# A relational graph layer: the first block keeps its edges, types come by marks, and the bias lies in PSUM

## The chip, the cores and the metric

The kernel runs on one core of one Trainium2 chip, in one launch. The metric is the device time of that launch in microseconds (us), a median of several runs; lower is better. TensorE (PE) multiplies matrices, VectorE (DVE) works elementwise, ScalarE (ACT) applies functions, GpSimd (POOL) here issues the gathers, and SyncE (SP) issues the other transfers.

## The reference

There are N = 12,500 nodes with 256 features each, E = 212,500 edges sorted by their target, and R = 8 relation types. Each node has one edge to itself, and it is the last of the node's edges in the sorted order.

```python
h   = relu(layernorm(x))                      # [12500, 256]
hx  = einsum('ni,rio->rno', h, weight)        # a 256x256 weight for each type
msg = hx[edge_type, src]
agg = segment_sum(msg, dst, num_segments=12500)
out = x + agg * sqrt(0.5) + h_bias + (h @ loop_weight) * sqrt(0.5)
```

## The kernel before

**Order of the sums.** The kernel sums first and multiplies later: for each type r and node d it adds the rows h[src] of the edges of that type, and then multiplies the eight sums of a node by the eight weights. The sums lie transposed in SBUF in `acc`, [128 features, 2 halves, 8 types, a ring of 768 nodes]. A *group* is 128 nodes; the ring has six slots (`SLOTS`), and 98 groups pass through it. Four groups make a quad (`XG = 4`), in which rows are loaded and stored.

**Tiles and units.** Edges are cut, in their order, into 796 units of 267 (`EDGES`). A unit takes two tiles (`PAIR`) of 128 message slots, 256 in all. It holds 267 edges because last edges that are self edges need no slot: they are taken out of the list (*compaction*), as their message is the node's own row. 128 units form a block (*b*, 7 of them), whose indices are prepared together, one unit per partition. `prepare(b)` lists the steps: `load_indices` (three transfers on SP: `nat_s`, `nat_d`, `nat_t`), `sources` (compaction in five rounds of two DVE operations, L331 and L332, then the transposed gather indices `gidx`), `last_edges` (the types of the last edges, compacted to the front in nine rounds: `loops`), `columns` (the column that each edge adds into) and `places`. These steps are put in a list called `background`, and some of them are taken from it at each tile.

**The main loop over 1592 tiles.** The order of the work on each engine is written out by hand. At tile t the loop issues `gather(t + 58)` on POOL (L607: 128 rows by index from HBM into `msg`, a buffer of 31 pairs of tiles), makes one-hot matrices for later tiles on DVE (L620: `oh` compares `cols` with a row of numbers), multiplies message by one-hot on PE (`edge_sums`, L647, two products of 32-bit floats, each of two instructions), and adds a unit's result into `acc` on DVE (`add_sums`, L659, at an offset held in a register).

**Rows.** Before it can gather from h, the kernel normalizes all rows (`norm_rows`, pieces of four times 128 rows: moments on DVE at L555 and L557, scaling on ACT at L567, then a store to h). Four pieces go ahead of the loop, the others in its first 28 tiles, three in four tiles. The first 96 tiles gather from x, and their messages are normalized as they come (`moments` with "e_").

**Groups.** When a group's last unit is in, `group_work(g)` puts 18 products (a self product and eight types, two halves each: L758, 36 instructions) and ahead of them a bias product (L752: a row of ones times `bias_in`) into a queue that is spread over the coming tiles. `finish()` then adds x (L767), stores a quad's output, and calls `begin(g + 6)`: two transposes of the new group's rows on PE (L671), a copy on ACT (`self_t`, L674), and eight DVE operations (L679) that set each type's columns of the slot to the row where the node's last edge has that type, and to zero elsewhere. `begin` thus both clears the slot and adds the last edges.

**Types.** `find_types(q)` gets, for a quad, the type of each node's last edge onto all 128 partitions. For each block that can touch the quad it makes one matrix of places on DVE (L698), and multiplies it by 22 columns of `loops`, each shifted by one (L701: 22 products of 128x512 elements for each block, 44 where two blocks touch the quad). ACT copies the result to `types` (L706). The transposes, the products for types and the turned indices share one PSUM bank, `ptt`, `pst` and `ptr` by name. Ahead of the loop the kernel runs block 0's preparation, `find_types` for the first two quads, and six `begin`s.

Of the kernel before, what the change touches and what calls it, by code (L numbers as in the profile page):

```python
# [28 lines left out]
EDGES = 267  # L29

# [6 lines left out]
SLOTS = 6  # L37
RING = GROUP * SLOTS

# [21 lines left out]
PREP = 300  # L61
STEP = 3
# [5 lines left out]
class Plan:  # L68
# [5 lines left out]

    def __init__(self, N, E):
        U = EDGES
        self.NU = NU = -(-E // U)
        self.NT = NU * PAIR - (1 if E - (NU - 1) * U <= P else 0)
        slack = 6.5 * (E / 4) ** 0.5 / U + 1.0
        self.rate = rate = E / (N * U)  # L80

        self.low = [(1 / rate, -slack / rate), (1.1 / rate, -(1.5 + 0.1 * E / U) / rate)]
        self.high = [(1 / rate, slack / rate)]
        self.starts = list(range(0, N, GROUP))
        self.ends = self.starts[1:] + [N]
        self.NG = len(self.starts)
        self.last = [
            min([NU - 1, *(int((e + 2 - b) / a) + 1 for a, b in self.low)]) for e in self.ends]
        self.last[-1] = NU - 1

        self.begin = lambda u: max(0.0, *(a * u + b for a, b in self.low))
        self.blocks = [
            [b for b in range(-(-NU // P))
             if self.begin(b * P) <= e + 2
             and self.high[0][0] * min(NU - 1, b * P + P - 1) + self.high[0][1] + 2 * WIN + 2 >= s]
            for s, e in zip(self.starts[::XG], self.starts[XG::XG] + [N])]
        a, b = self.high[0]
        self.first = [max(0, int((s - WIN - 2 - b) / a) - 1) if s else 0 for s in self.starts]
# [102 lines left out]
def kernel(  # L201
# [23 lines left out]
    EU = E - (NU - 1) * EDGES  # L225
    NB = -(-NU // P)

    TB, SB = (R - 1).bit_length(), (WIN - 1).bit_length()
# [12 lines left out]
    bias_in = const.tile([1, D], F32, name="bias_in")  # L241
    one = const.tile([1, P], F32, name="one")
# [5 lines left out]
    line = const.tile([P, XG * GROUP + WIN - 1], F32, name="line")  # L248
# [9 lines left out]
    with ExitStack() as main:  # L258
# [11 lines left out]

        selves = main.enter_context(tc.tile_pool(name="selves", bufs=SLOTS + 1))
# [9 lines left out]
        ps_o = main.enter_context(tc.tile_pool(name="ps_o", bufs=2, space=PSUM))  # L281
        msg, oh, offsets, kind = {}, {}, {}, {}
        firsts, loops, typed, gidx, col = {}, {}, {}, {}, {}
        added, begun = {}, set()
# [3 lines left out]
        def load_indices(b):  # L288
            rows_ = min(P, NU - b * P)
            last = b == NB - 1  # L290
            full = rows_ - last
            e0 = b * P * EDGES
            nat = {}
            for name, a, more in (("s", src, 0), ("d", dst, 1), ("t", etype, 0)):
                n = ep.tile([P, EDGES + more], I32, name=f"nat_{name}")
                if last:
# [4 lines left out]
                    else:  # L301
                        nc.vector.memset(n, 0)
                if full:
                    nc.sync.dma_start(n[:full, :], bass.AP(
                        tensor=a.tensor, offset=a.offset + e0, ap=[[EDGES, full], [1, EDGES + more]]))
# [21 lines left out]
        def compacted(got, bit, bits):  # L327

            def step(k):
                m = work_tile(got, "moves", 6, I32)  # L330
# [6 lines left out]
        def sources(b, got):  # L337


# [15 lines left out]
            def codes():  # L355
                nc.vector.scalar_tensor_tensor(
                    got["code"], got["code"], float(R), got["t"], op0=ALU.mult, op1=ALU.add)

            def packs():
                nc.vector.scalar_tensor_tensor(  # L360
                    packed, got["s"], float(1 << (TB + SB)), got["code"],
                    op0=ALU.mult, op1=ALU.add)

            def unpacks():
                nc.vector.tensor_single_scalar(
                    work_tile(got, "from", 6, I32)[:, :U], packed[:, :U], TB + SB,
# [11 lines left out]
        def last_edges(b, got):  # L378

            def selves_():  # L380
                nc.vector.tensor_tensor(
                    work_tile(got, "same", 4), got["s"], got["d"][:, :EDGES], op=ALU.is_equal)

            def ends():
                nc.vector.scalar_tensor_tensor(
                    work_tile(got, "end", 5), got["rise"], 1.0, got["same"],
# [7 lines left out]
            def codes():  # L394
                nc.vector.scalar_tensor_tensor(
                    got["rise"], got["rise"], -2.0 * R, got["t"], op0=ALU.mult, op1=ALU.add)
# [6 lines left out]
            def number():  # L403
                got["ends"] = small.tile([P, 1], F32, name="ends")
                nc.vector.tensor_reduce(got["ends"], got["end"], AX.X, ALU.add)

            def kept():
                nc.vector.tensor_single_scalar(
                    work_tile(got, "kinds", 6, I32)[:, :WIN], packed[:, :WIN], 2 * R - 1,
                    op=ALU.bitwise_and)  # L410
                loops[b] = small.tile([P, WIN], BF16, name="loops")
                nc.vector.scalar_tensor_tensor(
                    loops[b], line[:, :WIN], got["ends"], got["kinds"][:, :WIN],
                    op0=ALU.is_lt, op1=ALU.mult)

            return [selves_, ends, moves, codes, packs, number,
                    *compacted(got, TB + 1, (EDGES - 1).bit_length()), kept]

        def columns(b, got):
# [4 lines left out]
            def bases():  # L424
                got["base"] = small.tile([P, 1], F32, name="base")
                nc.vector.tensor_scalar(
                    got["base"], firsts[b], low[:, b : b + 1], high[:, b : b + 1],
                    op0=ALU.max, op1=ALU.min)

# [48 lines left out]
            def all_():  # L478
                nc.vector.scalar_tensor_tensor(
                    got["valid"], got["ends"], float(WIN), got["valid"], op0=ALU.min, op1=ALU.add)  # L480
                nc.vector.tensor_tensor(
                    counts[:, b : b + 1], got["valid"], got["fit"], op=ALU.mult)

            return [bases, offs, fits, number, there, moved, to, final, valid, sum_, all_,
# [95 lines left out]
        def norm_rows(i):  # L580
# [4 lines left out]
            def rest():  # L585
                after()
                nc.sync.dma_start(rows_of(h32, i), xt[:n, :k, :])
                for g in range(d // P, min(d // P + k, SLOTS, plan.NG)):
                    begin(g, xt[:, g - d // P, :])
# [65 lines left out]
        def add_sums(u, ps):  # L655
# [5 lines left out]

            assert all(g in begun for g in range(plan.NG) if plan.first[g] <= u)


        def begin(g, rows_):

            n = plan.ends[g] - plan.starts[g]
# [322 lines left out]
```

## Time and profile before

| | |
|---|---|
| Median of 3 runs | 2237.54 us (2236.86 to 2239.26) |
| Profiled execution | 2238.67 us |
| Its span on the core | 2236.7 us |
| Mean granted TensorE clock | 0.94 |
| Instructions | 30,467 |
| Bytes moved | 279.14 MB, of which 208.77 MB by the gathers' queue |
| First gather starts | 13.15 us |
| First edge product starts | 83.83 us |
| Bias load issued (all rows normalized) | 187.20 us |
| Last gather starts | 2151.26 us |

The page of a profile has the busy time of each engine, the chain of work that ended last followed back from the end, and the costliest groups of instructions by line: their busy time, the mean ns of one, and, behind the bar, the idle time of the engine just before them with what ended it. Lines of the timeline give a start, a duration, the engine, the line, output and inputs, and in brackets the idle time ahead with its releaser. Lines of the windows view give a stretch of time, its length, the busy time of PE, PE's weight loads, DVE, ACT and POOL, then the granted TensorE clock, the mean share of the transfer queues and GB/s. Idle time marked "issue" is time in which the engine waited for nothing that the profile shows.

### The profile page before, as it was taken

How to read it: one execution, taken by the hardware profiler on the slowest of the kernel's cores; microseconds unless marked ns; L12 is line 12 of the kernel's file. 1: busy time of each engine (PE TensorE's matmuls, PEld its weight loads, DVE VectorE, ACT ScalarE, POOL GpSimd, SP SyncE). 2: the span in 40 equal slices, each digit the busy share in tenths (PEclk: the TensorE clock that was granted, in tenths of full speed). 3: DMA queues.
4: the chain of work that ended last, by engine and by line, in shares of the span. 5: the costliest groups of instructions: out<-in, count | busy, mean ns of one | idle time of the engine just before them, and what ended most of it. 6: DMA issues, size and time to landing. Idle time of an engine off the chain costs nothing.

```text
span 2236.7 us, 30467 instructions
## 1 busy us (share of the span) xinstructions
PE 1984.4 (89%) x11073; PEld 1699.8 (76%) x11073; DVE 1290.3 (58%) x3124; ACT 170.4 (8%) x373; POOL 1512.0 (68%) x1618
## 2 busy tenths in 40 slices
PE   2236899999999999999999999999999799999999
PEld 1235788787787787797787797787797687897897
DVE  6787754485464485454584454684455475564552
ACT  1465300000000000000000000000000000000000
POOL 6624677676777677776777776777777576777730
PEclk9556999999999999999999999999999899999999
DMA  4785344343344344344343443444344343443420
GB/s 133 227 277 183 90 132 135 96 133 117 110 133 132 99 134 121 113 133 118 114 134 108 125 134 103 135 133 119 115 135 120 94 130 96 134 133 101 129 68 14
DMA packets 145685, 279.14 MB, mean 125 GB/s; under 512 B 27909, under 2 KB 94590, under 8 KB 145534
## 3 DMA queue, kind: packets, MB, share of 16 engines
q0 software_dynamic: 76416, 208.77, 32.3%
q1 hardware_dynamic: 69118, 68.40, 9.6%
q8 instruction: 90, 1.47, 0.3%
q14 instruction: 61, 0.50, 0.1%
HBM read 251.46 MB, written 25.60 MB: 124 GB/s over the span
## 4 chain that ended last, share of the span: by engine, by line
PE 78%; DVE 13%; issue 3%; ACT 2%; POOL 1%; DMA 1%; DVEq 0%; SPq 0%; ACTq 0%; POOLq 0%
PE ps L647 34%; PE po L758 31%; PE ptt L701 9%; DVE acc L679 4%; PE po L752 2%; DVE oh L620 1%; POOL msg L607 1%; DVE acc L659 1%; DVE moves L331 1%; PE pst L671 1%; DVE fixed L332 1%; DVE e_stats L555 1%; DVE n_stats L555 1%; ACT xt L567 1%; ACT self_t L674 0%
## 5 line engine op out<-in xcount | busy, mean ns | idle before, releaser
L607 POOL DMA_INDIRECT msg<-h,gidx x1496 | 1417.4, 947 | 544.8 <-issue 405.9
L647 PE MATMUL ps<-oh,msg 128*128 128x176 f32 (+1 forms) x6368 | 1103.7, 305 | 79.9 <-ACT msg L567 51.7
L647 PEld LDWEIGHTS ps<-oh,msg 128*128 128x128 f32 x6368 | 1028.6, 194 | 154.3 <-ACT msg L567 54.8
L758 PE MATMUL po<-w,acc 128*128 128x256 f32 x3136 | 870.2, 380 | 0.8 <-DVE flag L521 0.8
L620 DVE TENSOR_TENSOR oh<-fixed,cols 128x704 f32<-128x704 f32 x398 | 353.3, 888 | 445.4 <-PE ps L647 439.9
L659 DVE TENSOR_TENSOR acc<-acc,ps 128x352 f32 x796 | 409.3, 514 | 285.4 <-PE ps L647 278.9
L758 PEld LDWEIGHTS po<-w,acc 128*128 128x128 f32 x3136 | 531.8, 190 | 22.8 <-issue 1.0
L679 DVE SCALAR_TENSOR_TENSOR acc<-types,pst 128x256 f32<-128x256 bf16 (+1 forms) x784 | 267.5, 413 | 113.7 <-ACT self_t L674 113.7
L701 PE MATMUL ptt<-places,loops 128*128 128x512 bf16 (+1 forms) x748 | 210.7, 452 | 95.6 <-DVE places L698 94.9
L701 PEld LDWEIGHTS <-loops 128*128 128x128 bf16 x748 | 83.3, 114 | 217.2 <-DVE places L698 99.1
L674 ACT ACTIVATE self_t<-pst 128x256 f32<-128x256 f32 x98 | 37.4, 382 | 1578.5 <-PE pst L671 1578.5
L607 POOL DMA_INDIRECT msg<-in_x_dram,gidx x96 | 92.3, 962 | 94.7 <-issue 60.7
L758 PE MATMUL po<-wl,self_t 128*128 128x256 f32 x392 | 111.7, 408 | 0.0
L758 PEld LDWEIGHTS po<-wl,self_t 128*128 128x128 f32 x392 | 66.7, 190 | 38.2 <-issue 32.9
L752 PE MATMUL po<-bias_in,one 1*128 1x256 f32 x196 | 68.6, 429 | 0.9 <-DVE xr L767 0.9
L567 ACT ACTIVATE xt<-xt,n_shift,n_rstd 128x256 f32<-128x256 f32 x98 | 51.0, 589 | 29.8 <-DVE n_shift L564 29.8
L567 ACT ACTIVATE msg<-msg,e_shift,e_rstd 128x256 f32<-128x256 f32 x96 | 49.8, 589 | 13.4 <-DVE e_shift L564 13.4
L752 PEld LDWEIGHTS po<-bias_in,one 1*128 1x128 f32 x196 | 28.9, 184 | 23.3 <-issue 21.4
L767 DVE TENSOR_TENSOR xr<-xr,po 128x256 f32<-128x256 f32 x98 | 40.3, 412 | 9.1 <-PE po L758 8.7
L331 DVE TENSOR_SCALAR moves<-fixed 128x267 int32<-128x267 int32 x98 | 42.3, 431 | 2.1
L332 DVE COPY_PREDICATED fixed<-moves,fixed 128x266 int32<-128x266 int32 (+6 forms) x98 | 39.3, 401 | 3.4
L706 ACT ACTIVATE types<-ptt 128x512 bf16<-128x512 f32 (+1 forms) x25 | 14.7, 587 | 322.7 <-PE ptt L701 322.7
(92 smaller groups left out, 327.5 us busy)
## 6 DMA issues: line engine op xcount, KB each, us to landing
msg<-h,gidx POOLq DMA_INDIRECT x1496, 2.8
xt<-in_x_dram SPq DMA_DIRECT2D x24, 512.0 KB, 6.2
h<-xt SPq DMA_DIRECT2D x24, 512.0 KB, 3.8
xr<-in_x_dram SPq DMA_DIRECT2D x24, 512.0 KB, 7.7
out_dram<-xr SPq DMA_DIRECT2D x24, 512.0 KB, 3.6
hr<-h SPq DMA_DIRECT2D x23, 512.0 KB, 5.2
w<-in_L_gnn_weight_dram SPq DMA_DIRECT2D x2, 1024.0 KB, 5.9
msg<-in_x_dram,gidx POOLq DMA_INDIRECT x96, 2.9
```

Source lines behind the costliest of these rows:

```text
L331: nc.vector.tensor_single_scalar(m, packed, 1 << (bit + k), op=ALU.bitwise_and)
L332: nc.vector.copy_predicated(packed[:, : EDGES - (1 << k)], m[:, 1 << k :], packed[:, 1 << k :])
L555: nc.vector.bn_stats(stats[:n, j, :], rows_[j])
L567: nc.scalar.activation(rows_[j], rows_[j], AF.Relu, bias=shift[:n, j : j + 1], scale=rstd[:n, j : j + 1])
L607: nc.gpsimd.indirect_dma_start(out=msg[t], out_offset=None, in_=table[:, :], in_offset=bass.IndirectOffsetOnAxis(ap=gidx[b][:, at : at + 1 ...
L620: nc.vector.tensor_tensor(o[:, k : k + v, :i, :], iota_f.unsqueeze(1).unsqueeze(1).to_broadcast([P, v, i, C]), of.unsqueeze(3).to_broadcas ...
L647: nc.tensor.matmul(ps[:, c, from_ : from_ + width], m[:, c * P : (c + 1) * P], o[:, :width], start=(i == 0 and c == 0), stop=(end and c == ...
L659: i = nc.vector.tensor_tensor(a, a, ps, op=ALU.add)
L679: i = nc.vector.scalar_tensor_tensor(acc[:, :, r, s0 : s0 + n], of, float(r + 1), pst[:, :, :n], op0=ALU.is_equal, op1=ALU.mult)
L701: nc.tensor.matmul(pt[:, :n], loops[b][:, k : k + 1].to_broadcast([P, P]), o[:, WIN - 1 - k : WIN - 1 - k + n], start=(b == bs[0] and k == ...
L752: nc.tensor.matmul(got["out", g][:n], one[:, :n], bias_in, start=True, stop=False)
L758: i = nc.tensor.matmul(got["out", g][:n], lhs, rhs, start=False, stop=(r == R - 1 and c == KC - 1))
```

## The change

It has five parts.

1. Block 0 keeps all its edges: its units hold 256 edges, and self edges are gathered as all others are. No compaction, no last edges and no types are needed for it. There are then 802 units and 1603 tiles.
2. Quads that only block 0 can touch (the first three, `plan.typed = 3`) get no `begin`. Their slots of `acc` are cleared on ACT (`clear`; three ahead of the loop, three in its first tiles, six later), and their rows are loaded from h and transposed for the self product shortly before it (`turn_nodes`).
3. For the later quads, `mark` makes for each block two step functions over the quad's 512 nodes (from the first node of a unit, from the node behind its last). `find_types` multiplies them, as weights, by 24 columns (22 types and the unit's first node in two parts), 8 products for a block; six small DVE operations pick each node's type out of the result, and ACT scales the identity by it. Three tiles later `spread_types` multiplies a matrix of ones by this diagonal: one product of 128x512.
4. The bias is loaded onto all partitions and copied once into the second half of the two PSUM banks of the outputs. `finish` adds it with a DVE operation of its own, and the bias products are gone. The two banks are fixed ones, as the two rotating buffers were before.
5. Preparation of a block begins 184 tiles ahead instead of 300 (three steps in two tiles instead of three), so block 1 is prepared from tile 72 instead of tile 0.

In the changed kernel's numbering, edge products are L723, `add_sums` L735, the group's products L883, the small products L800 and the large one L825. The diff, cut to its core:

```diff
-        U = EDGES
-        self.NU = NU = -(-E // U)
+        U = PAIR * P
+        first = P * U
+        self.NU = NU = -(-E // U) if E <= first else P + -(-(E - first) // EDGES)
...
+        self.typed = min([q for q, b in enumerate(self.blocks) if b], default=len(self.blocks))
...
         def sources(b, got):
+            if b == 0:
+                def copy():
+                    nc.vector.tensor_copy(work_tile(got, "sf", 2)[:, :U], got["s"][:, :U])
+                return [copy, *turned(
+                    got, "sf", lambda: gidx.setdefault(b, idx.tile([P, U], I32, name="gidx")))]
...
         def last_edges(b, got):
+            if b == 0:
+                return []
...
+        def clear(g):
+            s0 = g % SLOTS * GROUP
+            a = acc[:, :, :, s0 : s0 + GROUP].rearrange("p c r d -> p (c r) d")
+            i = nc.scalar.activation(a, zero.unsqueeze(2).to_broadcast([P, KC * R, GROUP]), AF.Copy)
+            zeroed[g, "slot"] = i.ins
...
+        def mark(q):
             while any(b not in loops for b in plan.blocks[q]):
                 background.pop(0)[1]()
+            marked[q] = []
+            for k, b in enumerate(plan.blocks[q]):
+                m = marks.tile([P, 2, XG * GROUP], BF16, tag=f"mark{k}", name="mark")
+                for i, edge in enumerate((firsts[b], stops[b])):
+                    nc.vector.tensor_scalar(
+                        m[:, i, :], line, edge, float(-plan.starts[XG * q]),
+                        op0=ALU.subtract, op1=ALU.is_ge)
+                marked[q].append((b, m))
+
+        def find_types(q):
...
-                for k in range(WIN):
+            for g in range(XG):
+                for b, m, i in parts:
                     nc.tensor.matmul(
-                        pt[:, :n], loops[b][:, k : k + 1].to_broadcast([P, P]),
-                        o[:, WIN - 1 - k : WIN - 1 - k + n],
-                        start=(b == bs[0] and k == 0), stop=(b == bs[-1] and k == WIN - 1))
+                        pt[:, g, :], m[:, i, g * GROUP : (g + 1) * GROUP], loops[b][:, i, :],
+                        start=(b, m, i) == parts[0], stop=(b, m, i) == parts[-1])
...
+        def spread_types(q):
+            pt = ps_d.tile([P, 512], F32, tag="pt", name="ptt")
+            nc.tensor.matmul(pt, ones_b, marked.pop(q), start=True, stop=True)
             typed[q] = types.tile([P, XG * GROUP], BF16, name="types")
-            nc.scalar.activation(typed[q][:, :n], pt[:, :n], AF.Copy)
+            nc.scalar.activation(typed[q], pt, AF.Copy)
...
                 if (r, c) == (R, 0):
-                    got["out", g] = ps_o.tile([P, D], F32, name="po")
-                    nc.tensor.matmul(
-                        got["out", g][:n], one[:, :n], bias_in, start=True, stop=False)
+                    got["out", g] = outs[g % 2][:, 0, :]
...
                 rows_ = got["x", q]
+                nc.vector.tensor_add(rows_[:n, k, :], rows_[:n, k, :], outs[g % 2][:n, 1, :])
                 nc.vector.tensor_add(rows_[:n, k, :], rows_[:n, k, :], got["out", g][:n])
...
                 if b < plan.NG:
-                    begin(b, got["h", b // XG][:, b % XG, :])
...
+                    if q < plan.typed:
+                        clear(b)
+                    else:
+                        begin(b)
...
+            if q < plan.typed:
+                work.append((0.4, lambda: turn_nodes(g, early)))
...
-PREP = 300
-STEP = 3
+PREP = 184
+STEP = 2
```

## The prediction

> **What bounds the kernel now.** I read the page's parts 1, 4 and 5 first, for what fills the span.
>
> ```profile
> PE 1984.4 (89%) x11073; PEld 1699.8 (76%) x11073; DVE 1290.3 (58%) x3124; ACT 170.4 (8%) x373; POOL 1512.0 (68%) x1618
> ...
> PE 78%; DVE 13%; issue 3%; ACT 2%; POOL 1%; DMA 1%; DVEq 0%; SPq 0%; ACTq 0%; POOLq 0%
> ...
> L607 POOL DMA_INDIRECT msg<-h,gidx x1496 | 1417.4, 947 | 544.8 <-issue 405.9
> ...
> L701 PE MATMUL ptt<-places,loops 128*128 128x512 bf16 (+1 forms) x748 | 210.7, 452 | 95.6 <-DVE places L698 94.9
> ...
> L752 PE MATMUL po<-bias_in,one 1*128 1x256 f32 x196 | 68.6, 429 | 0.9 <-DVE xr L767 0.9
> ```
>
> PE is 89% busy and 78% of the chain that ended last, and the change removes two PE groups whole: 210.7 us (and 94.9 us of waiting for DVE) of type products, and 68.6 us of bias products. But POOL's gathers show 0.947 us busy and as much as 0.36 us idle "issue" each, so POOL may be fuller than 68%. The next view, POOL's timeline, says how full.
>
> ```profile
> 13.15 1.11 POOL L607 DMA_INDIRECT msg<-in_x_dram,gidx  x1 [10.58 <-DVE bound_o L820]
> 14.57 0.95 POOL L607 DMA_INDIRECT msg<-in_x_dram,gidx  x1 [0.30 <-issue]
> ...
> 210.75 0.95 POOL L607 DMA_INDIRECT msg<-h,gidx  x1 [4.25 <-ACT e_rstd L559]
> ...
> 1530.14 0.94 POOL L607 DMA_INDIRECT msg<-h,gidx  x1 [2.28 <-PE ps L647]
> ...
> 2151.26 0.95 POOL L607 DMA_INDIRECT msg<-h,gidx  x1 [0.30 <-issue]
> ```
>
> Each gather holds POOL for 0.95 us, and 0.30 us stands before the next whatever happens. Over the timeline, the idle time beyond that 0.30 us adds up to 145 us in the 1592 gathers; (2151.3 - 13.2 - 145) / 1591 = 1.253 us per gather when nothing holds it. So POOL is within 7% of being the limit itself: about 75 us of the 145 lie before 260 us (start-up), the other 70 come in lumps of 1 to 13 us that end on "PE ps", mostly right after a run of L701. PE is some 58 tiles behind throughout (the last gather starts at 2151.3, its product at 2222.6), which is the whole buffer of messages; POOL waits whenever PE gives a buffer back late.
>
> The windows view prices the start and the clock.
>
> ```profile
> 100.00:110.00 10.00, 2.81 (x9) 2.49 (x10) 9.01 (x39) 6.93 (x17) 3.13 (x4) 0.50 0.98 320
> 110.00:120.00 10.00, 3.71 (x12) 2.91 (x11) 8.66 (x38) 6.82 (x16) 2.08 (x3) 0.50 0.99 318
> ...
> 460.00:480.00 20.00, 17.13 (x100) 14.88 (x100) 19.17 (x52) 0.38 (x1) 15.13 (x17) 1.00 0.60 184
> ...
> 500.00:520.00 20.00, 16.12 (x75) 10.43 (x74) 7.13 (x16) 0.98 (x2) 9.38 (x10) 0.83 0.23 67
> ```
>
> While rows are normalized, the transfers reach 320 GB/s at a 0.98 share of the queues, and DVE is 90% busy: two near-limits at once. The last two rows are for the clock, below.
>
> **The change part by part.** The sum goes along POOL, in three pieces: when gather 104 starts (from which POOL last ran freely, at 210.75 us), the 1498 gathers behind it, and the tail. The tile count comes from the plan's arithmetic: 128 units of 256 edges and 674 of 267 make 1603 tiles instead of 1592.
>
> *PE's steady work.* From 336 to 2100 us POOL issued 1356 gathers, one each 1.30 us, all that PE let it; with 16.3 tiles to a group of 128 nodes that is 21.2 us per group. Removed per group: 0.69 us (one bias product in PE's timeline) and (210.7 + 94.9) / 98 = 3.1 us. Added: 216 small products (8 in each of 17 quads with one block, 16 in each of 5 with two). Their bounds are one weight load of L701, 0.114 us, and a whole old product in a dense run, 6.6/22 = 0.30 us: 25 to 65 us; I take 0.15, since they have 24 columns instead of 512, so 32 us. With 22 large products at 0.30, that is 0.4 us per group. The first small product still has to wait until begin's eight DVE operations have read the one PSUM bank that they share (2.9 us in the chain before an L701 run): 2.9 x 22 / 98 = 0.65. PE then needs about 21.2 - 0.7 - 3.1 + 0.4 + 0.65 = 18.4 us per group. POOL needs 16.3 x 1.253 = 20.4. **POOL becomes the bound**, and what PE gains beyond 0.8 us per group is not seen.
>
> *DVE and ACT.* DVE was 997 us busy in those 1764 us, 12.0 us per group. It gains 0.41 us per group (the bias add, as L767's add) and about 0.8 (marks at 0.5 us, a chain of six small operations): 13.2 of 20.4 in all, hidden under POOL. Behind the bias add stand the next one-hots and sums, which are made several tiles ahead. Were nothing to cover it, 98 x 0.41 = 40 us. The twelve groups of the first three quads get a clear on ACT instead of begin; its price lies near the 1.91 us that ACT took to scale a 128x2048 weight tile, on an engine that is 8% busy. Their transposes only move (0.38 us), now ahead of their own products. The old add waited for the group's last product (8.7 us over two waits in all), and the bias add is taken to wait for it too, at no cost in the sum. The Trainium skill, "PSUM — Partial Sum Buffer" (PSUM bank collisions raise a hardware error), asks for such a wait, as PE writes and DVE reads one bank; no run here shows a collision.
>
> *Opening.* PE's first edge product starts at 83.83 us. Ahead of it DVE's timeline has 8.6 us of compaction before block 0's indices, 11.0 us for its last edges, then two runs of L701 (33 to 46 us), and six begins amid four pieces of normalization (51 to 77 us). All of this goes. A copy, two transposes and a cast stay ahead of the first gather: about 5 us instead of 13.15. DVE reaches the first moments at 33.4 - 8.0 - 11.0 - 1.2 (shorter columns) + 1 (longer bounds) = 14 us. Six units of moments and scaling follow at 2.7 us (the spacing of such units near 95 to 103 us): first product at 30 us.
>
> *Until all rows are normalized.* Before, 83.8 to 187.2 us (the bias load is queued behind the last rows), 103 us, with block 1's index work in it: some 22 us of DVE operations and 7.1 us of waiting for nat_d. Both move to tile 72, and three clears add about 3 us on ACT: 77 us, so 107. But transfers have a say: 25.6 MB of rows and about 90 gathers of 131 kB are 37.4 MB, at 320 GB/s 117 us, plus 2 us at the start and some 3 us before the queues fill: 122 us. I take 122, with 107 (DVE alone) and 135 (the loop as long as before) as ends. Then, as before, 23.5 us from there to gather 104 (weights, first rows of h; SP has one more half-megabyte load of h in line, and PE's first transposes wait for it; 0 to 8 us): **145 us** instead of 210.75.
>
> *The rest.* 1498 x 1.253 = 1877. To it I add 10 us for stalls while PE's lag is still the whole buffer, above all at tiles 72 to 103, where block 1's index work falls among the last batches (bounds 0 and 25: a similar crowd at 440 to 500 us cost PE some 5 us). Block work later on stalls PE, not POOL, once the lag is gone; at 20.4 - 18.4 = 2.0 us per group the lag of 58 x 1.25 us is gone within 37 groups. Eleven more gathers (14 us) are in this count. Last gather at 145 + 1877 + 10 = 2032.
>
> *Tail.* Without lag the last tile lands about 3.5 us after its gather starts. PE still has the last products of group 96 between the last tiles and all of group 97, at 36 instructions in 9 us each: about 17.5 us behind the landing. Then an add and the store as now (2232.8 to 2236.7): 25 us in all, where before it was 85.
>
> Span 2057; the profiled execution took 2238.7 for a span of 2236.7 and the median was 2237.5, so about 2 us come on top of the span, within the spread of the median: **2059 us**. With the ends of the terms (145: 127 to 166; stalls 0 to 25; tail 20 to 32) it lies between 2040 and 2100.
>
> **The clock**, which speaks against idle PE time: the 460 to 480 row has PE 86% busy in short gaps at a clock of 1.00; in the 500 to 520 row (81% busy, with one long gap, of the kind that the timeline shows as 3.7 us ahead of an L701 run) it is 0.83. Fed by POOL, PE waits once a tile, at most 0.7 us, so I expect above 0.95. The Trainium skill, "TensorE: Matmul & The Clock Gate" (HAM oscillation — how this bites in real kernels), holds that gaps beyond about 3.4 us halve the clock; by that rule the sum stays as it is, and 22 such gaps would cost some 3 us each of PE time that POOL covers.
>
> **The rivals.**
>
> *PE stays the bound (12%).* The large product waits for marks, six DVE operations and four on ACT; if that chain is late, with other DVE work in its way, PE idles up to some 7 us per quad and its waits at L701 come back under another name. For it: DVE ended 94.9 us of PE's waits there. Against: the chain has three tiles' time. PE then needs 18.4 + 7/4 + 0.35 = 20.5 us per group: 145 + 96 groups left x 20.5 + 16 for the tail = 2129.
>
> *The start keeps its length (13%).* The window rows at 0.98 show little room, and if contention makes the loop take 103 us and the next steps 40, gather 104 comes at 175: 2089.
>
> *Slower (4%):* PE, no longer saturated, is granted a lower clock through the whole steady stage, as in every row with PE under half busy (0.50). It decides below 18.4/21.2 = 0.87 of full; at 0.75 a group takes 24.5 us, 145 + 96 x 24.5 + 16 = 2513. Against: a slower PE fills its own gaps, and rows without gaps show 1.00.
>
> The change doing less than it says is in the first rival. The forecast keeps 71%.
>
> **How the numbers follow.** The range holds nearly all of the forecast's own range (2040 to 2100) and the short start, and reaches toward the first rival: 2040 to 2115. Only the clock case is slower; a gain under 0.2% (4.5 us, about what a measurement here can tell) would need PE's gain nearly gone: faster 0.95, same 0.01, slower 0.04.
>
> **What would show it.** Right: POOL's gathers at 1.25 us almost without stalls after 250 us; PE's idle time at L723 ending on the msg transfers; the page's chain led by POOL instead of PE; first edge product near 30 us, gather 104 near 145; last product within 6 us of the last gather. Wrong: POOL still stalled by "PE ps" in lumps, PE above 90% busy after 336 us, a clock under 0.9, or the bias load later than 140 us.

## The result, and the profile after

The changed kernel takes 2106.9 us (median of 4 runs, 2100.5 to 2108.7) where the kernel before takes 2237.2 in the same comparison: a ratio of 0.9411 [0.9391, 0.9432]. Its profiled execution took 2107.2 us for a span of 2105.2. The forecast was 2059 us, so the gain is there, but 48 us of it are missing. The sum of the prediction went along POOL in three pieces, and they can be read off the trace in the same way (us from the span's start):

| | before | forecast | after |
|---|---|---|---|
| First edge product | 83.83 | 30 | 26.44 |
| Bias load issued | 187.20 | 122 | 113.44 |
| Gather 104 starts | 210.75 | 145 | 142.0 |
| Last gather ends | 2152.2 | 2033 | 2036.7 |
| End of the span | 2236.7 | 2057 | 2105.2 |
| Tail behind the last gather | 84.5 | 25 | 68.5 |

The first edge product, gather 104 and the last gather came out within 4 us of the forecast, and the tail did not. The page of after has the same parts as before: busy times, chain, and three groups of instructions.

```profile
PE 1789.1 (85%) x10411; PEld 1644.1 (78%) x10411; DVE 1327.7 (63%) x3274; ACT 218.5 (10%) x470; POOL 1523.2 (72%) x1630
...
PE 67%; DVE 13%; issue 6%; DMA 6%; POOL 4%; ACT 2%; SPq 0%; DVEq 0%; ACTq 0%; POOLq 0%
...
L683 POOL DMA_INDIRECT msg<-h,gidx x1507 | 1430.0, 949 | 481.7 <-issue 396.3
...
L800 PE MATMUL ptt<-loops,mark 128*128 128x24 bf16 x216 | 9.3, 179 | 80.8 <-DVE acc L773 80.8
L366 DVE TENSOR_TENSOR rise<-nat_d 128x267 f32<-128x267 int32 x6 | 2.6, 432 | 79.0 <-DMA nat_d<-in_dst_dram 79.0
```

PE lost 195 us of work, and the gathers' idle time fell from 544.8 to 481.7 us, of which 396 is the fixed gap. The row that has no place in the prediction is the last: six short operations on DVE, 2.6 us of work, with 79 us of waiting ahead of them. The timeline finds that wait; these are lines of four engines of after, in order of time (start, duration, engine, line, operation, and in brackets the idle time ahead with its releaser):

```profile
1710.60 0.26 SPq L325 DMA_DIRECT2D nat_s<-in_src_dram  x1
...
1782.61 0.37 POOL L317 IOTA nat_d<- 128x268 int32 x1
1783.00 0.29 SPq L322 DMA_DIRECT2D nat_d<-in_dst_dram  x1
...
1784.86 0.44 DVE L366 TENSOR_TENSOR rise<-nat_d 128x267 f32<-128x267 int32 x1 [74.36 <-DMA nat_d<-in_dst_dram]
1787.02 1.51 PE L723 MATMUL ps<-oh,msg 128*128 128x176 f32 x4 [66.64 <-DVE acc L735]
```

The last block has fewer units than partitions, so `load_indices` first fills its index tiles. Two are filled by a memset on DVE; `nat_d` is filled by an iota on POOL (L317), in both kernels. POOL's order is written by hand with the gathers 58 tiles ahead, so the iota stands behind 58 gathers for tiles that DVE and PE have not reached. SP issues `nat_s` at 1710, but the load of `nat_d` must wait for the iota, at 1782.6. DVE works in order and waits 74.36 us, and PE stands for 66.64 us. By the gather's own price that is the distance: 58 x 1.253 = 72.7 us. POOL meanwhile fills every message buffer; from there on PE is a whole buffer behind again, which it does not make up before the end.

The theory that I set out to test: **this iota costs after some 50 to 60 us, because the change let PE catch up with POOL.** While PE is 58 tiles behind, POOL has long been past the iota, and the wait is short. The rival: the tail is PE's ordinary lag, never made up, and the iota only moves idle time about.

Two groups of runs fell on slower chips: on one the kernel before takes 2778 us, on the other 2799. For those, ratios to the kernel before on the same chip are given, and times are compared only within one chip, unless the text says otherwise.

### The profile page after: what moved, and what is told of

Same layout as the page of the kernel before. It is cut to its first block, busy times and chain, and to the rows that moved or that the text cites. A ratio compares the mean times of both kernels' runs of the same rounds, so it can differ in the third digit from the quotient of the medians.

```text
span 2105.2 us, 29382 instructions
## 1 busy us (share of the span) xinstructions
PE 1789.1 (85%) x10411; PEld 1644.1 (78%) x10411; DVE 1327.7 (63%) x3274; ACT 218.5 (10%) x470; POOL 1523.2 (72%) x1630
## 4 chain that ended last, share of the span: by engine, by line
PE 67%; DVE 13%; issue 6%; DMA 6%; POOL 4%; ACT 2%; SPq 0%; DVEq 0%; ACTq 0%; POOLq 0%
PE ps L723 34%; PE po L883 31%; DMA msg<-h,gidx 4%; POOL msg L683 4%; DVE acc L773 3%; DVE acc L735 2%; DVE moves L349 2%; DVE fixed L350 2%; DMA h<-xt 1%; ACT xt L645 1%; DVE oh L696 1%; PE pst L759 1%; DMA w<-in_L_gnn_weight_dram 1%; DVE n_stats L633 0%; PE ptt L800 0%
## 5 line engine op out<-in xcount | busy, mean ns | idle before, releaser
L683 POOL DMA_INDIRECT msg<-h,gidx x1507 | 1430.0, 949 | 481.7 <-issue 396.3
L723 PE MATMUL ps<-oh,msg 128*128 128x176 f32 (+1 forms) x6412 | 1146.2, 310 | 187.5 <-DVE acc L735 76.6
L723 PEld LDWEIGHTS ps<-oh,msg 128*128 128x128 f32 x6412 | 1056.2, 198 | 290.1 <-issue 100.9
L883 PE MATMUL po<-w,acc 128*128 128x256 f32 x3136 | 892.7, 387 | 0.0
L883 PEld LDWEIGHTS po<-w,acc 128*128 128x128 f32 x3136 | 547.4, 195 | 25.3
L735 DVE TENSOR_TENSOR acc<-acc,ps 128x352 f32 x802 | 412.9, 515 | 180.9 <-PE ps L723 171.9
L773 DVE SCALAR_TENSOR_TENSOR acc<-types,pst 128x256 f32<-128x256 bf16 (+1 forms) x688 | 234.8, 414 | 74.5 <-ACT self_t L762 73.0
L883 PE MATMUL po<-wl,self_t 128*128 128x256 f32 x392 | 121.2, 438 | 3.9 <-ACT self_t L762 2.4
L883 PEld LDWEIGHTS po<-wl,self_t 128*128 128x128 f32 x392 | 75.7, 214 | 11.9 <-ACT self_t L762 2.8
L800 PE MATMUL ptt<-loops,mark 128*128 128x24 bf16 x216 | 9.3, 179 | 80.8 <-DVE acc L773 80.8
L800 PEld LDWEIGHTS <-mark 128*128 128x128 bf16 x216 | 7.3, 101 | 85.7 <-DVE acc L773 85.7
L894 DVE TENSOR_TENSOR xr<-xr,po 128x256 f32<-128x256 f32 x98 | 40.4, 412 | 7.4 <-PE po L883 7.4
L895 DVE TENSOR_TENSOR xr<-xr,po 128x256 f32<-128x256 f32 x98 | 41.2, 421 | 3.4
L818 ACT ACTIVATE diagonal<-ident,kinds 128x128 bf16<-128x128 f32 x88 | 28.1, 390 | 113.8 <-DVE kinds L815 113.8
L759 PE MATMUL pst<-ident,hr 128*128 128x128 f32 x196 | 37.7, 274 | 0.4 <-DVE offs L586 0.2
```

The costliest lines, as they stand in the source:

```text
L683: nc.gpsimd.indirect_dma_start(out=msg[t], out_offset=None, in_=table[:, :], in_offset=bass.IndirectOffsetOnAxis(ap=gidx[b][:, at : at + 1 ...
L723: nc.tensor.matmul(ps[:, c, from_ : from_ + width], m[:, c * P : (c + 1) * P], o[:, :width], start=(i == 0 and c == 0), stop=(end and c == ...
L735: i = nc.vector.tensor_tensor(a, a, ps, op=ALU.add)
L759: nc.tensor.transpose(pst[:, c, :n], rows_[:n, c * P : (c + 1) * P], ident[:n, :n])
L773: i = nc.vector.scalar_tensor_tensor(acc[:, :, r, s0 : s0 + n], of, float(r + 1), pst[:, :, :n], op0=ALU.is_equal, op1=ALU.mult)
L883: i = nc.tensor.matmul(got["out", g][:n], lhs, rhs, start=(r == R and c == 0), stop=(r == R - 1 and c == KC - 1))
```

## Experiments

### The fill on VectorE

```diff
-                        nc.gpsimd.iota(
-                            n, pattern=[[2, EDGES + 1]], base=N - 2 * EU, channel_multiplier=0)
+                        nc.vector.tensor_scalar(
+                            n, line[:, : EDGES + 1], 2.0, float(N - 2 * EU),
+                            op0=ALU.mult, op1=ALU.add)
```

The first run was on the first of the slower chips.

> The changed kernel, with the last block's filler for nat_d (2j + N - 2*EU in each row) written by one DVE operation from the row of numbers instead of an iota on POOL. Theory (the iota stands in POOL's queue behind the gather of 58 tiles later, and PE and DVE, which have caught up with POOL, wait for it): DVE's 74 us wait on nat_d goes to under 10 us, PE is not thrown back, the last product ends within some 27 us of the last gather's start, time 2055 to 2068 us. Rival (the long tail is PE's own lag, which the wait only happens to sit in): the last gather as now, the tail still over 55 us, time 2095 to 2107.

Measured: 2548.31 us, a ratio of 0.9161 [0.9115, 0.9206], against 0.9411 for the change as it is, which was measured on another chip. VectorE's wait falls to 3.4 us, but PE lags again here for other reasons: the last edge product ends 69 us behind the start of the last gather, where the theory said 27, and the tail is 82 us. So this run does not test the tail. The same kernel on a chip of the usual pace:

> The same fill of the next index tile on VectorE, on a chip on which the kernel before takes its 2238 us. Theory (the iota on POOL makes the last block's index tile late and so the tail long): VectorE's wait for that tile falls from 74 us to under 10, POOL loses the stalls that followed it (about 10 of the 14.6 us after 1780), its last gather ends at 2020 to 2030 us, and the tail is the 25 us of the forecast: 2047 to 2057 us in all. Rival (the tail comes from PE's lag alone, whatever filled the tile): 2095 to 2107 us.

Measured: 2051.93 us (2047.51 to 2054.24), ratio 0.9177 [0.916, 0.9194], 55 us below the changed kernel and the fastest version here that has all its gathers. In the trace gather 104 starts at 140.3, the last gather ends at 2021.4, and the span ends at 2045.8: the tail is 24.4 us. The time, the wait and the last gather are inside what the theory said, and the rival's 2095 is out. The timeline of VectorE in this run, around the last block's indices:

```profile
1708.59 0.23 DVE L317 TENSOR_SCALAR nat_d<-line 128x268 int32<-128x268 f32 x1
1708.83 0.28 DVE L321 MEMSET nat_t<- 128x268 int32 x1
1712.56 0.44 DVE L367 TENSOR_TENSOR rise<-nat_d 128x267 f32<-128x267 int32 x1 [3.45 <-DMA nat_d<-in_dst_dram]
```

The wait fell from 74.36 to 3.45 us, and POOL has no stall of more than 1 us beyond its fixed gap after 212 us. The 14 us of stalls beyond the fixed gap that after shows past 1780 us are most of the 15 us by which the last gather is earlier.

### The same fill in the kernel before

The same edit at the same place in the kernel before.

> The kernel before, with the same filler on DVE instead of the iota on POOL. Theory: there PE runs 58 tiles behind POOL, so the iota is long done when DVE needs it (it waited 1.4 us for nat_d at 1760 us), and the time stays within 5 us of before. Rival (the iota is a cost of its own, lag or not): 30 to 60 us less, as in the changed kernel.

Measured: 2227.39 us, ratio 0.9941 [0.9921, 0.9961], so 10.6 us (0.6%) faster. That is a miss for "within 5 us", and much less than the rival. The wait of 1.4 us that the expectation speaks of is not in the trace; the kernel before already shows a longer one, in its timeline:

```profile
1761.57 0.44 DVE L341 TENSOR_TENSOR rise<-nat_d 128x267 f32<-128x267 int32 x1 [9.98 <-DMA nat_d<-in_dst_dram]
...
1788.71 0.95 POOL L607 DMA_INDIRECT msg<-h,gidx  x1 [12.86 <-PE ps L647]
```

With the fill on DVE the 9.98 becomes 2.32 and POOL's stall of 12.86 becomes 4.59. The row was in the trace that the prediction was made from.

### The bias beside the outputs, alone

Part 4 of the change in the kernel before, nothing else.

```diff
+        outs = [ps_o.tile([P, 2, D], F32, name=f"po{i}") for i in range(2)]
...
-                    got["out", g] = ps_o.tile([P, D], F32, name="po")
-                    nc.tensor.matmul(
-                        got["out", g][:n], one[:, :n], bias_in, start=True, stop=False)
+                    got["out", g] = outs[g % 2][:, 0, :]
...
+                nc.vector.tensor_add(rows_[:n, k, :], rows_[:n, k, :], outs[g % 2][:n, 1, :])
```

> The kernel before with the bias part alone: bias copied once beside the outputs in PSUM, added by DVE, no bias products. Theory (PE is the bound there, POOL is close behind): PE saves 0.69 us per group, 68 us in all, of which POOL's 70 us of stalls after the start leave room for most: time 2165 to 2185. Rival (DVE's extra read waits or collides, or POOL takes the gain away at once): 2215 to 2240.

Measured: 2181.07 us, ratio 0.974 [0.9724, 0.9756]: 57 us less, or 0.58 us per group, inside the theory. And the same wait grew, as the timelines of VectorE and TensorE of this run show:

```profile
1721.75 0.44 DVE L341 TENSOR_TENSOR rise<-nat_d 128x267 f32<-128x267 int32 x1 [25.46 <-DMA nat_d<-in_dst_dram]
1723.91 3.87 PE L647 MATMUL ps<-oh,msg 128*128 128x176 f32 x16 [19.99 <-issue]
```

DVE's wait is 9.98 us in before, 25.46 with PE 0.58 us per group lighter, and 74.36 with the whole change; PE stands 4.18, 19.99 and 66.64 us behind it. How far PE is behind POOL when the wait begins can be counted. Kept to the tile `msg`, the windows view has the number of edge products begun (four for a tile) in brackets behind PE's time, and the number of gathers behind POOL's. These are before, this run and after, each from the start to the beginning of the wait:

```profile
0.00:1751.00 1751.00, 857.43 (x4938) 798.92 (x4939) 33.51 (x96) 49.78 (x96) 1222.21 (x1289) 0.93 0.44 132
```

```profile
0.00:1696.00 1696.00, 860.30 (x4940) 801.11 (x4941) 33.56 (x96) 49.78 (x96) 1211.69 (x1277) 0.93 0.46 135
```

```profile
0.00:1710.00 1710.00, 967.54 (x5402) 890.84 (x5403) 33.53 (x96) 49.65 (x96) 1283.83 (x1353) 0.93 0.47 141
```

PE is 54.5, 42 and 2.5 tiles behind. Against before, 12.5 and 52 tiles of lag are gone, which at 1.253 us make 15.7 and 65.2 us; the wait is longer by 15.5 and 64.4. One instruction, in the same place on POOL, costs more the better PE keeps up, by what is gone of the lag.

### The bias product back on TensorE

The fill on VectorE and part 4 undone, all else as changed.

```diff
+                    nc.tensor.matmul(
+                        got["out", g][:n], ones[0:1, :].to_broadcast([1, n]), bias_in, start=True, stop=False)
...
-                nc.vector.tensor_add(rows_[:n, k, :], rows_[:n, k, :], outs[g % 2][:n, 1, :])
```

On the first of the slower chips:

> The kernel with the filler on DVE, and the bias part undone: a bias product (one row of ones times the bias, 0.69 us on PE for each group) opens each group's products again, and the DVE add of the bias is gone. Theory (POOL is the bound at 20.4 us per group, PE needs about 18.4): PE goes to 19.1 us, still under POOL, so the time is that of the kernel with the filler on DVE within 5 us. Rival (PE is still the bound): 98 x 0.69 = 68 us more.

Measured: ratio 0.9288 [0.9256, 0.9321], 1.3 points above the fill alone and 33 us slower there, a miss for "within 5 us". On a chip of the usual pace:

> The fill on VectorE and the bias product back on PE as before, all else as changed, on a chip of the same pace. Theory (POOL is the bound, and PE has 1 to 2 us per group to spare, which the bias product takes up): PE needs about as long as POOL, so 10 to 35 us more than with the fill alone, nearly all of it at the end as lag of PE. Rival (PE is still the bound): 49 blocks of bias products times their 1.1 to 1.2 us, 55 us more.

Measured: 2066.08 us, ratio 0.924 [0.9222, 0.9257], 14 us more than with the fill alone, where the same edit was worth 57 us in the kernel before. The trace says where: the last gather ends at 2018.1, 3 us earlier than with the fill alone, and the tail is 44 us instead of 24. The products, 76.4 us of busy time, hide under POOL's pace except for the lag that is left at the end.

### The old products for the types

The fill on VectorE and part 3 undone: 22 shifted products for each block of a quad.

```diff
+                for k in range(WIN):
+                    nc.tensor.matmul(
+                        pt[:, :n], loops[b][:, 0, k : k + 1].to_broadcast([P, P]),
+                        o[:, WIN - 1 - k : WIN - 1 - k + n],
+                        start=(b == bs[0] and k == 0), stop=(b == bs[-1] and k == WIN - 1))
```

On the first of the slower chips:

> The kernel with the filler on DVE, and the type part undone for the later quads: 22 shifted products of 128x512 for each block, and no marks, small products or diagonal. Theory: PE's quad is then 79 to 85 us (82 to 88 before, less four bias products), POOL's is 81.6, so PE never makes up its lag of 58 tiles: the last gather starts near 2040 and the tail is about 80 us, time 2105 to 2130. Rival (the types were off the critical path, or the start-up gave the whole gain): within 10 us of the kernel with the filler on DVE.

Measured: ratio 0.9627 [0.9588, 0.9666], 4.7 points above the fill alone. On a chip of the usual pace:

> The fill on VectorE and the old 22 shifted products for the types, all else as changed, on a chip of the same pace. Theory: the start gets its idle stretch on PE back, the first edge products and the bias load come later, POOL starts its steady stretch later by that much: 60 to 90 us more than with the fill alone. Rival (the types' products lie beside other work anyway): within 10 us of it.

Measured: 2108.79 us, ratio 0.9425 [0.9407, 0.9443], 57 us more than with the fill alone. The size is just under the theory's 60 to 90, and its reason is wrong. The bias load is issued at 113.6 us and gather 104 starts at 142.4, as with the new products: the first three quads touch only block 0 and need no types at all, so nothing comes back at the start. The loss is at the end, 12 us on the last gather and 52 on the tail (76 us), 64 between the two profiled executions. Of this run, from the page's groups:

```profile
L794 PE MATMUL ptt<-places,loops 128*128 128x512 bf16 (+1 forms) x573 | 165.6, 452 | 94.4 <-DVE places L791 90.9
```

260 us of products and waits here stand against 90 us for L800 in after (and 8 for the large product); POOL's pace hides two thirds of the difference.

### Half of the gathers

The fill on VectorE, and the second tile of a unit multiplies the messages of the first, so that half of the gathers from h are left out. The work of PE and DVE stays, the sums are other ones.

```diff
+            if kind[t] == "h" and t % PAIR:
+                msg[t] = msg[t - 1]
+                return
```

On the first of the slower chips:

> The kernel with the filler on DVE, leaving out every second gather from h: the second tile of a unit multiplies the first tile's messages, so the sums are not the reference's; PE's and DVE's work is the same. Theory (POOL is the bound): POOL needs 10.2 us per group and PE becomes the bound again at its own 18 to 18.5 us per group: 145 + 96 x 18.3 + 16, time 1890 to 1930 us, PE over 95% busy after 300 us. Rival (PE or DVE is the bound, POOL just follows): 2050 to 2070 as with all gathers.

Measured: 2051.65 us in one run, 497 us below the fill alone on that chip. On a chip of the usual pace:

> The fill on VectorE, and every odd tile takes the messages of the even tile before it, so that half the gathers of h are left out. On a chip of the same pace. Theory (POOL's gathers are the bound, PE's 18.4 us per group are next): PE sets the time, 98 groups at 18.4 us and the start of some 100 to 130 us: 1890 to 1950 us. Rival (PE is already the bound): within 20 us of the run with all gathers.

Measured: 1986.67 us in one run (span 1984.9), 61 us below the span with all gathers, but 37 us above the upper end of the theory. So POOL does set the time, and PE is closer behind it than I had thought. The gathers' group of this run, and the page's chain and gathers' group with the fill alone:

```profile
L687 POOL DMA_INDIRECT msg<-h,gidx x754 | 716.6, 950 | 1055.3 <-PE ps L727 939.6
```

```profile
PE 67%; DVE 12%; DMA 8%; issue 6%; POOL 4%; ACT 2%; SPq 0%; DVEq 0%; ACTq 0%; POOLq 0%
...
L684 POOL DMA_INDIRECT msg<-h,gidx x1507 | 1429.6, 949 | 467.2 <-issue 398.2
```

With half of them POOL waits 940 us for PE's buffers; with all of them it waits almost only for its own fixed gap. The chain of the second kernel still gives POOL 4%, although 1498 x 1.253 us = 1877 us of its time are gathers back to back (1881 measured from gather 104 on). Presumably, as PE pauses only briefly for a tile, the walk back mostly goes from one PE instruction to the one before it. The run with half the gathers also gives PE's own pace: the first self product of group 16 starts 1428 us before that of group 90, 19.3 us per group, where all gathers give 20.0 (20.5 from group 44 on, POOL's own pace) and the kernel before 21.2.

### Block 1 prepared from tile 0

The fill on VectorE, `PREP = 300` and `STEP = 3` instead of 184 and 2: part 5 undone.

> The kernel with the filler on DVE, and the fifth part undone: block preparation begins 300 tiles ahead in steps of three tiles, so block 1's index work lies in the first tiles again, among the normalization. Theory (DVE and ACT in lockstep set the pace there): the bias load is issued 20 to 29 us later than the 113 us of the changed kernel, and the time grows by as much. Rival (transfers set the pace, at 370 GB/s and a share above 1.0 in these windows): under 10 us later.

Measured: 2069.71 us, ratio 0.9249 [0.9233, 0.9264]. The bias load is issued at 134.4 us instead of 112.2, gather 104 starts at 163.4 instead of 140.3, and the span ends at 2067.5 instead of 2045.8. (The medians lie 18 us apart; the profiled execution of the fill alone was its fastest.) The theory's 20 to 29 us hold for the bias load, and the rival's 10 are out. What is lost in the start, 23 us at gather 104, is lost at the end, 22: nothing behind it gives time back, which is what a bound at a fixed pace does.

### The first block alone

Parts 1, 2 and 5 with the fill on VectorE; the old products and the bias product are both back (the two edits above together).

> Parts 1, 2 and 5 of the change alone (block 0 keeps its edges, cleared slots, later preparation), with the fill on VectorE; the 22 shifted products and the bias product are back on PE. Theory (the price of the same PE work depends on who is the bound: beside the small products POOL was, and the bias products cost 14 us; with the old products PE is): the bias products cost here what they cost the kernel before, about 57 us more than the run with the old products alone: 2155 to 2175 us, with POOL's stalls in lumps that end on PE. Rival (the bias product is worth 14 us in any company): 2118 to 2128 us. The start is as long as with the whole change: first edge product near 26 us and bias load near 113 us.

Measured: 2738.41 us on the second of the slower chips, ratio 0.978 [0.9729, 0.9831]. It is 1.5 points above the old products alone, which ran on the first; that is some 42 us at such a pace, with intervals about a point wide. With the small products the bias products cost 33 us on the first. Scaled by the chip (2799 / 2237) the theory said about 71 and the rival 17, so this tells neither. The start can be compared between the two: the bias load is issued at 173.8 us here, and on the first chip at 173.2 to 173.3 with the three versions that have all gathers. On the usual chip it is issued at 112.8 us with the old bias and at 113.6 with the old products, against 187.2 before. The short start thus needs neither the new products nor the new bias; it comes with the first block and the later preparation.

## Why the prediction was right, and where it failed

**The time: in the range by luck.** 2106.9 us lies in the range of 2040 to 2115 that was given, but outside the 2040 to 2100 of the forecast's own terms (whose ends, added up, make 2026 to 2102). The range reached that far only for the first rival, which is not what happened. 55 us come from one wait that no term has, and without it the time is 2051.9.

**The bound: right.** POOL sets the pace with 1.253 us per gather: from gather 104 to the end of the last the run with the fill on VectorE took 1881 us, where the prediction had 1877 for the gathers and 10 for stalls. With half of the gathers 61 us go, and PE's own 19.3 us per group are below POOL's 20.4; the first rival (PE stays the bound, at 20.5) is out.

**The start: right.** Gather 104 at 142 against 145, first edge product at 26.4 against 30. The bias load came at 113.4, not 122, as the transfers do more than the 320 GB/s that I took: in the windows view of after,

```profile
50.00:100.00 50.00, 20.32 (x65) 17.66 (x66) 41.17 (x189) 41.23 (x89) 37.82 (x41) 0.50 1.07 373
```

373 GB/s at a share of 1.07. That the transfers alone set the time there is not shown, as block 1's index work moves the bias load by 22 us. Five of these 9 us were lost again in the next piece: from the bias load to gather 104 passed 28.6 us, not 23.5. The move of block 1's index work, for which the sum had 103 - 77 = 26 us with the clears, is worth 18 (medians) to 22 (spans) in the run that undoes it.

**The tail: the failed step.** The prediction said "Without lag the last tile lands about 3.5 us after its gather starts", and before that "Block work later on stalls PE, not POOL, once the lag is gone". The second sentence is true, and it is why the condition of the first did not hold: a stall of PE while POOL runs on *is* the lag. I priced every instruction that the change moves, but not the iota that stays where it was on POOL's queue. Its distance from its user, 58 tiles, had been hidden by a lag of nearly as many, and I removed the lag. With the iota gone the tail is 24.4 us, against 25 forecast, and the median 2051.9 against 2059. The step that was missing could have been written from the trace of before: 9.98 us of waiting for `nat_d` with a lag of 54 tiles, up to 58 x 1.25 us = 73 without.

**PE's pace: mis-sized.** I had 18.4 us per group, 2.8 less than before; the run with half of the gathers shows 19.3 from group 16 to group 90, 1.9 less. The groups of PE's instructions in that stretch say which terms were off. Of before (551.9 to 2117.6 us):

```profile
L647 PE MATMUL ps<-oh,msg 128*128 128x176 f32 (+1 forms) x4824 | 820.3, 300 | 7.2 <-issue 7.1
L701 PE MATMUL ptt<-places,loops 128*128 128x512 bf16 (+1 forms) x572 | 159.4, 450 | 76.0 <-DVE places L698 76.0
L318 PE MATMUL ptr<-ident,sf 128*128 128x128 f32 x8 | 1.6, 276 | 1.8 <-DVE acc L679 1.8
```

Of the run with half of the gathers (438.5 to 1867 us):

```profile
L727 PE MATMUL ps<-oh,msg 128*128 128x176 f32 (+1 forms) x4824 | 836.7, 304 | 9.1 <-issue 7.4 <-DVE acc L739 1.6
L804 PE MATMUL ptt<-loops,mark 128*128 128x24 bf16 x192 | 8.3, 181 | 75.7 <-DVE acc L777 75.7
L337 PE MATMUL ptr<-ident,sf 128*128 128x128 f32 x10 | 3.1, 412 | 23.3 <-DVE sf L394 23.3
```

The types came out near the sum: 235 us before, 91 now with the large products, 1.95 us per group less (2.05 in the sum). The small products are nearly free (9.3 us in all of after, not 32), PE waits longer for them (80.8 us, not 64). The bias products are the 0.7 us that they were taken for. Missing in the sum are two things. PE now waits 23 us for the turned block indices (0.3 us per group). And the same edge and group products take 1604 us instead of 1565 (0.5 us per group).

The lag, counted as above, is 59 tiles at 150 us of after, 30 at 450 and 4.5 at 1050, and PE first waits for messages from h at 983 us. From gather 104 that is 41 groups, where I had written 37. That this is so near is in part luck: until 450 us, mostly in the quads without types, 2.5 us per group are given back, then 1.1, and 2.0 in neither stretch.

Part of the 0.5 us is the clock. In after, waits of 3.31 and 7.17 us at L800 end at 710.7 and 796.6 us. The windows view of the 5 us behind each, and of the 5 us after that, has the granted clock third from the right:

```profile
710.00:715.00 5.00, 4.29 (x20) 3.75 (x21) 3.54 (x11) 1.28 (x4) 3.78 (x5) 0.66 0.37 105
715.00:720.00 5.00, 5.00 (x32) 4.64 (x31) 1.84 (x3) 0.60 (x1) 3.78 (x5) 1.00 0.37 108
```

```profile
796.00:801.00 5.00, 4.40 (x22) 3.94 (x23) 4.14 (x16) 1.28 (x4) 3.78 (x5) 0.59 0.38 107
801.00:806.00 5.00, 5.00 (x34) 4.66 (x32) 3.30 (x10) 0.60 (x1) 3.78 (x5) 1.00 0.35 99
```

A clock of 0.66 and 0.59 for 5 us loses 1.7 and 2.0 us, not the 3 that I had written beside the sum, then it is full again. Such dips are not new: before has them behind its waits at L701, and the 21.2 us from which the sum started hold them. From group 16 to group 90 the clock below 1.00 takes 48 us in before and 65 in the run with half of the gathers, so it explains at most 17 of the 40 us. The rest is not settled. The Trainium skill, "TensorE: Matmul & The Clock Gate" (HAM oscillation — how this bites in real kernels), has idle gaps beyond about 3.4 us throttle the clock; the trace agrees for the gap of 7.17 us, and shows the dip behind one of 3.31 us as well.

**DVE and ACT: right.** The bias adds take 41.2 us in all and wait 3.4; nothing in the trace waits long for them.

**The signs.** For "right", the two times of the start came, gathers at 1.25 us with 23 us of stalls in all, and PE's waits at L723 ending on messages (27.1 us in 41 waits). Two did not come: the chain stays with PE even where POOL sets the time, and the last edge product starts 54 us behind the end of the last gather, and still 10 us with the fill on VectorE. Of the signs for "wrong", two came as well: behind the iota's wait POOL is stalled by "PE ps" in lumps of up to 5.0 us, and PE is over 90% busy, 91% from 336 to 2020 us with the fill on VectorE, although POOL sets the pace there. So a busy PE was no sign of the bound. The granted clock in the steady stretches of after (340 to 1640 us) is 0.95 to 0.96, and the third rival is out. Its ground, 0.50 in every row with PE under half busy, was too wide: in the first 50 us of before PE is busy for 14.6 us at 0.99.

## What to carry to other kernels

When a change lets a late engine catch up, look for everything that the lag has hidden: any instruction queued on an engine that runs ahead, which feeds an engine that doesn't, waits for the whole distance once the lag is gone (58 gathers x 1.25 us here). A wait of a few microseconds on such a path in the trace of before is the warning, and its worst case is the run-ahead times the pace, not the wait that is seen. A part that is worth 57 us where its engine is the bound is worth 14 where the bound has moved on, and only a run with the other engine's work taken away shows how near the next bound is; the chain does not, and neither does a share of busy time.

## What the runs showed of the hardware that I had not expected

Chips can be slower for this kernel in a way that the granted clock does not explain: the kernel before took 2778 us on one and 2799 on another, 24 to 25% more, while on the first the mean clock of the fill alone was 0.885 instead of 0.939. One gather costs POOL the same there (951 ns), but its wait list has 171.6 us in 100 waits that end on another core or an unknown queue, and 240.9 us on PE's buffers. With half of the gathers the time there is 2051.65 us, 65 us above the other chip's, and 61 of these lie ahead of gather 104 (209.0 us against 147.7). From group 16 to group 90 a group then takes 19.3 us on both chips; with all gathers it takes 24.9 against 20.0. So the start is slower with or without half of the gathers, and the steady stage only with all of them. What it is stays open. A product of 128x24 with bf16 operands adds 43 ns to PE's busy time (9.3 us / 216), though the mean of its records is 179 ns: they lie over one another.
